# One scan for both channel tiles of a pair, and three VectorE steps one part further back in the queue

## The chip, the cores and the metric

The kernel runs on one core of one Trainium2 chip. The metric is the device time of one execution in microseconds. All data are 32-bit floats in on-chip memory (SBUF) and in the matmul accumulators (PSUM). TensorE is called PE below, VectorE DVE, ScalarE ACT, GpSimd POOL; SyncE (SP) issues most of the transfers.

## The reference

A decoder layer in three blocks, for 8 sequences of 512 tokens with 512 features: a selective state-space block (Mamba), cross-attention with 16 heads on a context of 512 tokens, and a mixture of 32 experts (4 of them chosen per token) with one shared expert; layer norms between them. The change touches the first block:

```python
x_main, z = jnp.split(layernorm(x) @ in_proj_w, 2, axis=-1)      # 1024 channels each
x_main = silu(causal_depthwise_conv1d(x_main, conv_w, conv_b))   # 4 taps
dt, B_ssm, C_ssm = split(x_main @ x_proj_w)                      # 32, 16, 16
dt = softplus(dt @ dt_proj_w + dt_proj_b)
dA  = exp(A[None, None] * dt[..., None])                         # 16 states per channel
dBx = dt[..., None] * B_ssm[:, :, None, :] * x_main[..., None]
h = dA_t * h + dBx_t                                             # step by step over the tokens
y = einsum('bdn,bn->bd', h, C_t) + x_main * D_param
out = (y * silu(z)) @ out_proj_w + x
```

In the gate of the experts, a rank of the 8 groups is computed by comparing them in pairs, and constant rows of numbers are added and multiplied in.

## The kernel before

The state-space block goes through 16 chunks: 8 sequences `b` times two halves `t` of `T` = 256 tokens. A chunk has 32 steps `k`, in the order `q`, `g`, `ci`: 4 pairs `q` of channel tiles, for each pair 4 groups `g` of 4 of the 16 states, and for each group the two channel tiles `ci` of the pair. A channel tile is 128 channels, and a tile of a step holds on its 128 partitions half of the channels for two states each, so that 4 rows of 256 tokens stand behind each other on a partition, each with one more element in front for the state carried in.

One step is made of:

- `carry` (L439): takes a buffer `h` of 4 rows of 257 elements (four such buffers in turn, `bufs=4`), and ACT copies the states carried in (or zeros, in the first half) to the front elements.
- `decays` (L433): four ACT exponentials fill one of the two tiles `l_da`, always one step ahead of its use.
- `scan` (L446): DVE multiplies `dtx` (the tile called `both` in the profile) by the broadcast states B (`bc[0]`) into `h` (L449), runs the recurrence over all 1028 elements in one scan instruction (L453; a zero of `l_da` in front of each row restarts it), and in the first half copies the 4 last states out (L455).
- `collect` (L457): DVE multiplies `h` by the broadcast states C (`bc[1]`, L470), and PE sums the states into the accumulator `py` with four matmuls (L474), which are eight records in the profile. With `g == 0` two more matmuls (L462) begin `py` with the skip connection.

After the 8 steps of a pair, `gated` (L482) multiplies the gate `zs` by `py`; there is one buffer of `py`. A buffer of `h` is free again when PE has summed it. `bcast` (L374) loads the states B and C one group ahead through SP's queue.

All else is cut into parts that run beside the scans: the input projections and convolution of the next chunk (`convolve`, L314, whose last three taps are DVE's `other_taps`, L335), the softplus of the next pair (`prepare`, L387, with its DVE part `both`, L410, which also issues eight transfers on SP's queue), the output projection, and the attention and gate of the sequence before (`units`). In attention, `maximum` (L758) makes two matmuls into a PSUM tile `ps_s` that DVE reduces to a maximum (`mx`, L768); `weigh` makes the scores `ps_t`, of which ACT makes exponentials; both share two PSUM buffers, and they take turns.

A part gives its matmuls at once and hands back what is to be done with the result. `do` (L992) runs a part and then calls `settle` (L983), which runs what the earlier parts left over; what that hands back waits for the next `settle`. So each further function handed back puts the work one part later. From this written order and its own dependencies, a scheduler in the framework makes the queue of each engine; the queues are worked off strictly in order.

Of the kernel before, what the change touches and what calls it, by code (L numbers as in the profile page):

```python
# [16 lines left out]
P = 128  # L17
# [64 lines left out]
def layers(ctx, tc, a, x1d, filld, based, xbuf):  # L82
# [73 lines left out]

    conv_tail = cp.tile([P, CC, 3], F32, name="l_conv_tail")
    state = cp.tile([P, CC, NST // NG, NG], F32, name="l_state")
    nothing = cp.tile([P, NG, 1], F32, name="l_nothing")
    nc.gpsimd.memset(nothing, 0.0)  # L160
    das = [cp.tile([P, NG, T + 1], F32, name=f"l_da{i}") for i in range(2)]
    for da in das:
        nc.gpsimd.memset(da[:, :, 0:1], 0.0)

# [23 lines left out]
        channel_multiplier=0,  # L188
    )

    early = cp.tile([P, SC, E], F32, name="l_early")
    nc.gpsimd.iota(
        early, pattern=[[0, SC], [-1, E]], base=E, channel_multiplier=0, allow_small_or_imprecise_dtypes=True
    )
    first = cp.tile([P, SC, E], F32, name="l_first")
    nc.gpsimd.iota(
        first, pattern=[[0, SC], [CAP, E]], base=-SLOTS, channel_multiplier=0, allow_small_or_imprecise_dtypes=True
    )

    taken = cp.tile([P, SC + 1, E], F32, name="l_taken")  # L200
    nc.gpsimd.memset(taken, 0.0)
# [112 lines left out]
    def convolve(t, q, f):  # L314

        c0 = 2 * q
        ps = project(f, "ps_x")

        def first_tap():
            xp = p1.tile([P, 2, T + 3], F32, tag="xp", name="xp")  # L320
            if t == 0:
                nc.gpsimd.memset(xp[:, :, 0:3], 0.0)
            else:
                nc.gpsimd.tensor_copy(xp[:, :, 0:3], conv_tail[:, c0 : c0 + 2, :])
            nc.scalar.copy(xp[:, :, 3:], ps)
            if t < S // T - 1:
                nc.gpsimd.tensor_copy(conv_tail[:, c0 : c0 + 2, :], xp[:, :, T : T + 3])
            f["xs"][q] = xs = p2.tile([P, 2, T], F32, tag="xs", name="xs", bufs=6)
            for i in range(2):
                c = c0 + i  # L330
                nc.scalar.activation(
                    xs[:, i, :], xp[:, i, 0:T], AF.Identity, bias=cb[:, c : c + 1], scale=cw[:, c, 0:1]
                )

            def other_taps():  # L335
                for i in range(2):
                    acc = xs[:, i, :]
                    for k in range(1, 4):
                        nc.vector.scalar_tensor_tensor(
                            acc, xp[:, i, k : k + T], cw[:, c0 + i, k : k + 1], acc, ALU.mult, ALU.add  # L340
                        )

            return other_taps

        return first_tap

# [27 lines left out]
    def bcast(f, g):  # L374

        got = []
        for r0 in (g * NG, NST + g * NG):
            t = bcp.tile([P, NG // 2, T], F32, tag="bc", name="bc")
            for r in range(2):
                n0 = r0 + r * NG // 2  # L380
                nc.sync.dma_start(
                    t[r * HP : (r + 1) * HP], f["scr"][n0 : n0 + NG // 2, :].partition_broadcast(HP)
                )
            got.append(t.unsqueeze(1).to_broadcast([P, 2, NG // 2, T]))
        return got

    def prepare(q, f):  # L387

        ps = psm.tile([P, 2, T], F32, tag="mm", name="ps_dt")
        for i in range(2):  # L390
            c = 2 * q + i
            nc.tensor.matmul(
                ps[:, i, :], w_dt[:, c * P : (c + 1) * P], f["xd"][0:RANK, :], start=True, stop=True
            )

        def exponentials():
# [11 lines left out]
            nc.scalar.activation(w, u, AF.Identity, bias=1.0)  # L408

            def both():  # L410

                nc.vector.scalar_tensor_tensor(w, w, -1.0, u, ALU.add, ALU.subtract)
                nc.vector.tensor_tensor(l, l, w, ALU.subtract)
                nc.vector.tensor_tensor(dt, dt, l, ALU.add)
                nc.vector.tensor_tensor(dtx, dt, f["xs"][q], ALU.mult)
                for i in range(2):
                    c = 2 * q + i
                    nc.scalar.activation(
                        f["xs"][q][:, i, :], f["xs"][q][:, i, :], AF.Identity, scale=dpar[:, c : c + 1]
                    )  # L420
                f["ready", q] = []
                for src in (dt, dtx):
                    to = p2.tile([P, 2, 2, T], F32, tag=f"both{len(f['ready', q])}", name="both")
                    for r in range(2):
                        for j in range(2):
                            nc.sync.dma_start(to[r * HP : (r + 1) * HP, :, j, :], src[j * HP : (j + 1) * HP])
                    f["ready", q].append(to)

            return both

        return exponentials

    def decays(c, g, dt, da):  # L433

        for n in range(NG):
            j, m = n // 2, n % 2
            nc.scalar.activation(da[:, n, 1:], dt[:, c % 2, j, :], AF.Exp, scale=aneg[:, c, j, g, m : m + 1])  # L437

    def carry(t, c, g):  # L439

        last = state[:, c, g].unsqueeze(2)
        h = p3.tile([P, NG, T + 1], F32, tag="h", name="h", bufs=4)
        nc.scalar.copy(h[:, :, 0:1], last if t else nothing)  # L443
        return h

    def scan(t, c, g, dtx, bc, da, h):  # L446

        steps = h.rearrange("p (j m) t -> p j m t", j=2)[:, :, :, 1:]
        nc.vector.tensor_tensor(  # L449
            steps, dtx[:, c % 2].unsqueeze(2).to_broadcast([P, 2, NG // 2, T]), bc[0], ALU.mult  # L450
        )
        flat = h.rearrange("p n t -> p (n t)")
        nc.vector.tensor_tensor_scan(flat, da.rearrange("p n t -> p (n t)"), flat, 0.0, ALU.mult, ALU.add)  # L453
        if t < S // T - 1:
            nc.vector.tensor_copy(state[:, c, g].unsqueeze(2), h[:, :, T : T + 1])  # L455

    def collect(c, g, h, bc, py, f):  # L457


        if g == 0:  # L460
            for j in range(2):
                nc.tensor.matmul(  # L462
                    py[j * HP : (j + 1) * HP, c % 2, :],
                    ident[:, j * HP : (j + 1) * HP],
                    f["xs"][c // 2][:, c % 2, :],
                    start=(c % 2 == 0),
                    stop=False,
                )
        steps = h.rearrange("p (j m) t -> p j m t", j=2)[:, :, :, 1:]
        nc.vector.tensor_tensor(steps, steps, bc[1], ALU.mult)  # L470
        for m in range(NG // 2):
            for j in range(2):
                s = (g, m, c % 2)
# [70 lines left out]
    def choose(b, x2t, pl, st):  # L544
# [13 lines left out]
        square = [P, SC, G, G]  # L558
        other = gs.unsqueeze(2).to_broadcast(square)
        own = gs.unsqueeze(3).to_broadcast(square)  # L560
        eq = gm.tile(square, F32, tag="g_eq", name="g_eq")
        nc.vector.tensor_tensor(eq, other, own, ALU.is_equal)
        nc.vector.tensor_tensor(eq, eq, lower.unsqueeze(1).to_broadcast(square), ALU.mult)
        gt = gm.tile(square, F32, tag="g_gt", name="g_gt")
# [458 lines left out]
    for i, (b, t) in enumerate(chunks):  # L1023
# [8 lines left out]
        for k, (q, g, ci) in enumerate(steps):  # L1032
            if ci == 0:
                if (q, g) != (CC // 2 - 1, NST // NG - 1):
                    bcn = bcast(f, (g + 1) % (NST // NG))
                else:
                    bcn = bcast(nf, 0) if after else None
            h = carry(t, 2 * q + ci, g)

            if k + 1 < len(steps) or after:  # L1040
                nq, ng, ni = steps[(k + 1) % len(steps)]
                decays(2 * nq + ni, ng, (f if k + 1 < len(steps) else nf)["ready", nq][0], das[(n + 1) % 2])
            scan(t, 2 * q + ci, g, f["ready", q][1], bc, das[n % 2], h)
            n += 1
            if k % 8 == 0:
                if k:
                    gated(q - 1, f, py)
                elif old:
                    gated(CC // 2 - 1, old[2], old[3])
                py = psy.tile([P, 2, T], F32, tag="py", name="py")  # L1050
            if k == 0 and old:
                twice_x(*old[:3])
            if k in (1, 2) and old:
# [365 lines left out]
```

## Time and profile before

| | |
|---|---|
| median of 3 runs | 5609.93 us (5609.75 to 5616.93) |
| the profiled execution's own time | 5620.06 us |
| its span, first to last instruction | 5617.3 us |
| busy in the span: PE / DVE / ACT / POOL | 4888.6 / 4351.5 / 2592.2 / 546.1 us |
| mean granted TensorE clock | 0.934 |

The profile counts an engine as busy while an instruction of it runs. A row of the groups gives the busy time, the mean length of one instruction in ns, and the idle time of the engine just before such instructions with what ended it. The busy time of PE is modelled and is not PE at its peak. The scans run from 84 us to 3724 us after the start; behind that lie the rest of the last sequence's attention, to about 4000 us, and then the experts and the final norm, in which nothing of the scan remains.

### The profile page before, as it was taken

What the parts mean: (1) busy time and instruction counts of PE and PEld (TensorE: products, weight loads), DVE (VectorE), ACT (ScalarE), POOL (GpSimd) and SP (SyncE); (2) the same over time, 40 slices, a digit from 0 to 9 for tenths busy, and PEclk for the clock granted to TensorE, in tenths of its full rate; (3) what the DMA queues carried; (4) which work ended last, traced back from release to release, by engine and by line L of the source; (5) the groups of instructions that cost most, each with busy time, mean ns of one, the idle gap of its engine ahead of it and who ended that gap; (6) DMA issues with size and microseconds to landing.
All of it is one profiled execution on the core that took longest, in us unless ns stands there. A gap on an engine that the chain in (4) does not pass through costs nothing. (4 is left out here: it accounts for less than half of the span.)

```text
span 5617.3 us, 60406 instructions
## 1 busy us (share of the span) xinstructions
PE 4888.6 (87%) x19752; PEld 2725.6 (49%) x19752; DVE 4351.5 (77%) x5738; ACT 2592.2 (46%) x5480; POOL 546.1 (10%) x424
## 2 busy tenths in 40 slices
PE   5667888888888988888888898879899999999994
PEld 3333344434433434443443443333577777777773
DVE  5988888989889998898989899854555655555554
ACT  4454555655556555565545656523122222222223
POOL 0000002001100200200010020010111111111111
PEclk8778999999999999999999999989899999999997
DMA  6777345434534534543463453431444444444444
GB/s 207 215 219 201 99 129 177 128 112 130 189 107 113 190 107 122 177 132 106 124 204 94 125 183 110 115 118 45 137 124 126 124 124 119 125 126 124 120 117 138
DMA packets 560426, 769.83 MB, mean 137 GB/s; under 512 B 135754, under 2 KB 268394, under 8 KB 560112
## 3 DMA queue, kind: packets, MB, share of 16 engines
q1 hardware_dynamic: 522608, 680.70, 40.2%
q0 software_dynamic: 33280, 76.90, 7.0%
q10 hardware_dynamic: 4224, 8.39, 0.4%
q8 instruction: 156, 2.56, 0.2%
q14 instruction: 158, 1.29, 0.1%
HBM read 508.68 MB, written 165.05 MB: 120 GB/s over the span
## 5 line engine op out<-in xcount | busy, mean ns | idle before, releaser
L437 ACT ACTIVATE l_da<-both,l_aneg 128x256 f32<-128x256 f32 x2048 | 888.4, 499 | 801.8 <-DVE h L453 759.7
L453 DVE TENSOR_TENSOR_SCAN h<-l_da,h 128x1028 f32<-128x1028 f32 x512 | 1171.2, 2295 | 48.5 <-ACT h L443 26.4
L474 PE MATMUL py<-h,l_twice 128*64 128x256 f32 x4096 | 628.1, 420 | 217.4 <-DVE h L470 217.3
L449 DVE TENSOR_TENSOR h<-both,bc 128x1024 f32<-128x1024 f32 x512 | 619.2, 1216 | 97.2 <-PE py L474 45.4
L470 DVE TENSOR_TENSOR h<-h,bc 128x1024 f32<-128x1024 f32 x512 | 623.5, 1220 | 6.0
L474 PEld LDWEIGHTS py<-h,l_twice 128*64 128x64 f32 x4096 | 295.3, 147 | 587.6 <-DVE h L470 260.7
L766 PE MATMUL ps_s<-l_ka,l_qa 64*128 64x512 f32 x1024 | 317.1, 699 | 142.9 <-DVE mx L768 142.7
L1199 PE MATMUL ps_h<-xT,w 128*128 128x320 f32 x1536 | 435.6, 433 | 0.0
L1279 POOL DMA_INDIRECT based<-y,xe x160 | 250.5, 1565 | 1317.2 <-ACT y L1302 579.9
L768 DVE TENSOR_REDUCE mx<-ps_s 128x2 f32<-128x1024 f32 x256 | 310.8, 1217 | 83.7 <-PE ps_s L766 82.9
L1220 DVE TENSOR_TENSOR hT<-ps_h,p 128x320 f32<-128x320 f32 x128 | 62.9, 492 | 374.7 <-PE ps_h L1199 374.6
L1199 PEld LDWEIGHTS ps_h<-xT,w 128*128 128x128 f32 x1536 | 292.4, 191 | 118.4 <-issue 0.8
L792 PE MATMUL ps_t<-l_qa,l_ka 64*128 64x512 f32 x1024 | 302.0, 654 | 15.8 <-ACT eT L796 11.9
L796 ACT ACTIVATE eT<-ps_t 128x1024 f32<-128x1024 f32 x256 | 259.1, 1013 | 111.9 <-PE ps_t L792 111.5
L808 PE MATMUL po<-eT,l_va 128*64 128x512 f32 x1024 | 279.2, 623 | 23.0 <-ACT raw L820 19.0
L1199 PE MATMUL ps_h<-t,s 128*128 128x320 f32 x1024 | 286.1, 432 | 0.0
L641 POOL DMA_INDIRECT xbuf<-x2t,dest x128 | 216.7, 1693 | 622.1 <-DVE dest L635 583.7
L305 PE MATMUL ps_z<-xnT,wm 128*128 128x256 f32 x1024 | 246.3, 395 | 31.2 <-DMA wm<-in_in_proj_w 28.4
L503 PE MATMUL po<-wm,zs 128*128 128x512 f32 x512 | 246.7, 634 | 13.0 <-DMA wm<-in_out_proj_w 8.5
L703 PE MATMUL ps_p<-x2T,wa 128*128 128x512 f32 x512 | 244.7, 627 | 11.1 <-DVE hT L883 9.1
L305 PE MATMUL ps_x<-xnT,wm 128*128 128x256 f32 x1024 | 245.3, 393 | 1.4 <-ACT xnT L294 1.1
L305 PEld LDWEIGHTS ps_z<-xnT,wm 128*128 128x128 f32 x1024 | 196.2, 196 | 83.7 <-ACT l_da L437 27.1
(225 smaller groups left out, 7397.0 us busy)
## 6 DMA issues: line engine op xcount, KB each, us to landing
bc<-scr SPq DMA_DIRECT2D x1024, 128.0 KB
w<-in_w SPq DMA_DIRECT2D x96, 1024.0 KB
wm<-in_in_proj_w SPq DMA_DIRECT2D x128, 512.0 KB
xbuf<-zero SPq DMA_DIRECT2D x32, 1362.5 KB
xe<-xbuf SPq DMA_DIRECT2D x32, 1362.5 KB
both<-dt SPq DMA_DIRECT2D x256, 128.0 KB
both<-dtx SPq DMA_DIRECT2D x256, 128.0 KB
wm<-in_out_proj_w SPq DMA_DIRECT2D x64, 512.0 KB
```

The costliest lines, as they stand in the source:

```text
L305: nc.tensor.matmul(ps[:, i, :], w[:, dc, i * P : (i + 1) * P], f["xnT"][:, dc, :], start=(dc == 0), stop=(dc == DC - 1),)
L437: nc.scalar.activation(da[:, n, 1:], dt[:, c % 2, j, :], AF.Exp, scale=aneg[:, c, j, g, m : m + 1])
L449: nc.vector.tensor_tensor(steps, dtx[:, c % 2].unsqueeze(2).to_broadcast([P, 2, NG // 2, T]), bc[0], ALU.mult)
L453: nc.vector.tensor_tensor_scan(flat, da.rearrange("p n t -> p (n t)"), flat, 0.0, ALU.mult, ALU.add)
L470: nc.vector.tensor_tensor(steps, steps, bc[1], ALU.mult)
L474: nc.tensor.matmul(py[j * HP : (j + 1) * HP, c % 2, :], twice, h[:, j * 2 + m, 1:], start=False, stop=(s == (NST // NG - 1, NG // 2 - 1, 1)),)
L766: nc.tensor.matmul(ps[:, j, :], qa[r, lt * P : (lt + 1) * P], ka[r, :], start=True, stop=True)
L768: return lambda: nc.vector.tensor_reduce(mx[:, lt, :].unsqueeze(2), ps, AX.X, ALU.max) and None
L792: nc.tensor.matmul(ps[:, j, :], ka[r, kc * P : (kc + 1) * P], qa[r, :], start=True, stop=True)
L796: nc.scalar.activation(eT, ps, AF.Exp)
L808: nc.tensor.matmul(po[j * 2 * HD : (j + 1) * 2 * HD, :], va[:, kc, i, j * HD : (j + 2) * HD], eT[:, j, :], start=(kc == 0), stop=(kc == SC ...
L1199: nc.tensor.matmul(ps, w[:, n, r * P : (r + 1) * P], x[:, n, :], start=not more and n == 0, stop=n == 1, skip_group_check=more,)
```

## The change

Five things are edited.

1. `carry`, `decays` and `scan` work on both channel tiles of a pair at once, at every even `k`: `h` and `l_da` have 8 rows of 257 elements, there are two buffers of `h` instead of four, and two of `l_da` as before. The decays are computed one pair of steps ahead. `collect` is as before, once for each channel tile, on half of `h`.
2. `other_taps` and `both` are handed back through one more function, so they come one part later.
3. `gated` stands just ahead of `collect`, behind the parts of the step, and not just behind the scan.
4. `prepare` is called at `k % 8 == 2`, not 3.
5. The constants `early` and `first` hold one row that is broadcast, and the two comparison tiles of the gate lie in one buffer of the shared tag `row`.

```diff
-    nothing = cp.tile([P, NG, 1], F32, name="l_nothing")
+    none = cp.tile([P, 2, NG], F32, name="l_none")
...
-    das = [cp.tile([P, NG, T + 1], F32, name=f"l_da{i}") for i in range(2)]
+    das = [cp.tile([P, 2 * NG, T + 1], F32, name=f"l_da{i}") for i in range(2)]
...
-    early = cp.tile([P, SC, E], F32, name="l_early")
...
+    early = early.unsqueeze(1).to_broadcast([P, SC, E])
...
-            return other_taps
+            return lambda: other_taps
...
-            return both
+            return lambda: both
...
+    def decays(q, g, dt, da):
+
+        for i in range(2):
+            for n in range(NG):
+                j, m = n // 2, n % 2
+                nc.scalar.activation(
+                    da[:, i * NG + n, 1:], dt[:, i, j, :], AF.Exp, scale=aneg[:, 2 * q + i, j, g, m : m + 1]
+                )
...
-        h = p3.tile([P, NG, T + 1], F32, tag="h", name="h", bufs=4)
-        nc.scalar.copy(h[:, :, 0:1], last if t else nothing)
+        h = p3.tile([P, 2 * NG, T + 1], F32, tag="h", name="h", bufs=2)
+        nc.scalar.copy(h.rearrange("p (i n) t -> p i n t", i=2)[:, :, :, 0], last(q, g) if t else none)
...
+        steps = h.rearrange("p (j m) t -> p j m t", m=NG // 2)[:, :, :, 1:]
+        both = [P, 4, NG // 2, T]
         nc.vector.tensor_tensor(
-            steps, dtx[:, c % 2].unsqueeze(2).to_broadcast([P, 2, NG // 2, T]), bc[0], ALU.mult
+            steps,
+            dtx.rearrange("p i j t -> p (i j) t").unsqueeze(2).to_broadcast(both),
+            bc[0].to_broadcast(both),
+            ALU.mult,
         )
         flat = h.rearrange("p n t -> p (n t)")
         nc.vector.tensor_tensor_scan(flat, da.rearrange("p n t -> p (n t)"), flat, 0.0, ALU.mult, ALU.add)
         if t < S // T - 1:
-            nc.vector.tensor_copy(state[:, c, g].unsqueeze(2), h[:, :, T : T + 1])
+            nc.vector.tensor_copy(last(q, g), h.rearrange("p (i n) t -> p i n t", i=2)[:, :, :, T])
...
+        h = h[:, c % 2 * NG : (c % 2 + 1) * NG]
         steps = h.rearrange("p (j m) t -> p j m t", j=2)[:, :, :, 1:]
-        nc.vector.tensor_tensor(steps, steps, bc[1], ALU.mult)
+        nc.vector.tensor_tensor(steps, steps, bc[1].to_broadcast([P, 2, NG // 2, T]), ALU.mult)
...
-        eq = gm.tile(square, F32, tag="g_eq", name="g_eq")
+        both = p3.tile([P, D], F32, tag="row", name="g_eq").rearrange("p (n j g h) -> p n j g h", n=2, j=SC, g=G)
+        eq, gt = both[:, 0], both[:, 1]
...
-            h = carry(t, 2 * q + ci, g)
-
-            if k + 1 < len(steps) or after:
-                nq, ng, ni = steps[(k + 1) % len(steps)]
-                decays(2 * nq + ni, ng, (f if k + 1 < len(steps) else nf)["ready", nq][0], das[(n + 1) % 2])
-            scan(t, 2 * q + ci, g, f["ready", q][1], bc, das[n % 2], h)
-            n += 1
-            if k % 8 == 0:
-                if k:
-                    gated(q - 1, f, py)
-                elif old:
-                    gated(CC // 2 - 1, old[2], old[3])
-                py = psy.tile([P, 2, T], F32, tag="py", name="py")
+            if ci == 0:
+                h = carry(t, q, g)
+
+                if k + 2 < len(steps) or after:
+                    nq, ng, _ = steps[(k + 2) % len(steps)]
+                    decays(nq, ng, (f if k + 2 < len(steps) else nf)["ready", nq][0], das[(n + 1) % 2])
+                scan(t, q, g, f["ready", q][1], bc, das[n % 2], h)
+                n += 1
...
-            if k % 8 == 3:
+            if k % 8 == 2:
                 if q + 1 < CC // 2:
                     do(prepare, q + 1, f)
...
             settle()
+            if k % 8 == 0:
+                if k:
+                    gated(q - 1, f, py)
+                elif old:
+                    gated(CC // 2 - 1, old[2], old[3])
+                py = psy.tile([P, 2, T], F32, tag="py", name="py")
             collect(2 * q + ci, g, h, bc, py, f)
```

More of the change, by code (lines that the diff above doesn't have):

```diff
@@ L158, in layers @@
     state = cp.tile([P, CC, NST // NG, NG], F32, name="l_state")
-    nothing = cp.tile([P, NG, 1], F32, name="l_nothing")
-    nc.gpsimd.memset(nothing, 0.0)
-    das = [cp.tile([P, NG, T + 1], F32, name=f"l_da{i}") for i in range(2)]
+    none = cp.tile([P, 2, NG], F32, name="l_none")
+    nc.gpsimd.memset(none, 0.0)
+    das = [cp.tile([P, 2 * NG, T + 1], F32, name=f"l_da{i}") for i in range(2)]
     for da in das:
@@ L189, in layers @@
     )
-    early = cp.tile([P, SC, E], F32, name="l_early")
[L192 to L198, printed above, removed]
+    early = cp.tile([P, E], F32, name="l_early")
+    nc.gpsimd.iota(early, pattern=[[-1, E]], base=E, channel_multiplier=0, allow_small_or_imprecise_dtypes=True)
+    early = early.unsqueeze(1).to_broadcast([P, SC, E])
+    first = cp.tile([P, E], F32, name="l_first")
+    nc.gpsimd.iota(first, pattern=[[CAP, E]], base=-SLOTS, channel_multiplier=0, allow_small_or_imprecise_dtypes=True)
+    first = first.unsqueeze(1).to_broadcast([P, SC, E])
     taken = cp.tile([P, SC + 1, E], F32, name="l_taken")
@@ L383, in bcast @@
                 )
-            got.append(t.unsqueeze(1).to_broadcast([P, 2, NG // 2, T]))
+            got.append(t.unsqueeze(1))
         return got
@@ L427, in both, with carry, last, scan @@
                     f["ready", q].append(to)
-            return both
+            return lambda: both
         return exponentials
[L433 to L441, printed above, removed]
-        h = p3.tile([P, NG, T + 1], F32, tag="h", name="h", bufs=4)
-        nc.scalar.copy(h[:, :, 0:1], last if t else nothing)
-        return h
-    def scan(t, c, g, dtx, bc, da, h):
-        steps = h.rearrange("p (j m) t -> p j m t", j=2)[:, :, :, 1:]
+    def decays(q, g, dt, da):
[5 more added lines that the diff above has]
+                )
+    def carry(t, q, g):
+        h = p3.tile([P, 2 * NG, T + 1], F32, tag="h", name="h", bufs=2)
+        nc.scalar.copy(h.rearrange("p (i n) t -> p i n t", i=2)[:, :, :, 0], last(q, g) if t else none)
+        return h
+    def last(q, g):
+        return state[:, 2 * q : 2 * q + 2, g]
+    def scan(t, q, g, dtx, bc, da, h):
+        steps = h.rearrange("p (j m) t -> p j m t", m=NG // 2)[:, :, :, 1:]
+        both = [P, 4, NG // 2, T]
         nc.vector.tensor_tensor(
-            steps, dtx[:, c % 2].unsqueeze(2).to_broadcast([P, 2, NG // 2, T]), bc[0], ALU.mult
+            steps,
+            dtx.rearrange("p i j t -> p (i j) t").unsqueeze(2).to_broadcast(both),
+            bc[0].to_broadcast(both),
+            ALU.mult,
         )
@@ L560, in choose @@
         own = gs.unsqueeze(3).to_broadcast(square)
-        eq = gm.tile(square, F32, tag="g_eq", name="g_eq")
+        both = p3.tile([P, D], F32, tag="row", name="g_eq").rearrange("p (n j g h) -> p n j g h", n=2, j=SC, g=G)
+        eq, gt = both[:, 0], both[:, 1]
         nc.vector.tensor_tensor(eq, other, own, ALU.is_equal)
         nc.vector.tensor_tensor(eq, eq, lower.unsqueeze(1).to_broadcast(square), ALU.mult)
-        gt = gm.tile(square, F32, tag="g_gt", name="g_gt")
         nc.vector.tensor_tensor(gt, other, own, ALU.is_gt)
```

## The prediction, made before the changed kernel ran

> **What bounds the kernel now.** I read the windows first, to see which stage the change reaches. All scans lie between 84 and 3724 us:
>
> ```profile
> core 0: us, PE busy (x) PEld busy (x) DVE busy (x) ACT busy (x) POOL busy (x), PEclk, DMA share, GB/s
> 84.00:3724.00 3640.00, 3094.19 (x12620) 1479.61 (x12620) 3299.42 (x3751) 2041.92 (x4353) 252.52 (x190) 0.92 0.49 144
> ```
>
> VectorE is busy for 3299 of 3640 us (91%), TensorE for 3094 (85%), ScalarE for 56%. So a microsecond off VectorE's queue counts here if TensorE follows, and nothing after 3724 us can change. Next the groups, for what a step costs:
>
> ```profile
> L453 DVE TENSOR_TENSOR_SCAN h<-l_da,h 128x1028 f32<-128x1028 f32 x512 | 1171.2, 2295 | 48.5 <-ACT h L443 26.4
> L449 DVE TENSOR_TENSOR h<-both,bc 128x1024 f32<-128x1024 f32 x512 | 619.2, 1216 | 97.2 <-PE py L474 45.4
> L455 DVE COPY l_state<-h 128x4 f32<-128x4 f32 x256 | 42.1, 166 | 2.9
> L413 DVE TENSOR_TENSOR l<-l,dtx 128x512 f32<-128x512 f32 x64 | 44.1, 688 | 1.0
> ```
>
> Then the waits of VectorE in those 3640 us (total, times, longest), to see what its 341 idle us are:
>
> ```profile
> DVE h L449 <- PE py L474: 45.4, 27, 3.7
> DVE zs L486 <- PE py L474: 40.2, 19, 4.3
> DVE xs L339 <- ACT xs L331: 33.0, 21, 4.7
> DVE dtx L412 <- ACT dtx L408: 27.0, 7, 5.2
> DVE h L449 <- DMA both<-dtx: 26.8, 15, 7.1
> DVE h L453 <- ACT h L443: 26.4, 16, 2.0
> ```
>
> No single wait rules. Two of them, 45.4 and 26.4 us, are the ring of `h` buffers: the multiply, or the ScalarE copy ahead of it, stands until TensorE has summed an old buffer. Three others (40.2, 33.0 and 27.0) belong to the instructions that edits 2 and 3 put back. Last the timeline, for how VectorE's instructions follow each other:
>
> ```profile
> 1583.17 1.22 DVE L449 TENSOR_TENSOR h<-both,bc 128x1024 f32<-128x1024 f32 x1
> 1584.49 2.30 DVE L453 TENSOR_TENSOR_SCAN h<-l_da,h 128x1028 f32<-128x1028 f32 x1
> 1586.82 0.17 DVE L455 COPY l_state<-h 128x4 f32<-128x4 f32 x1
> 1587.03 1.23 DVE L470 TENSOR_TENSOR h<-h,bc 128x1024 f32<-128x1024 f32 x1
> 1588.17 1.22 DVE L768 TENSOR_REDUCE mx<-ps_s 128x2 f32<-128x1024 f32 x1
> 1589.31 1.22 DVE L449 TENSOR_TENSOR h<-both,bc 128x1024 f32<-128x1024 f32 x1
> 1589.44 1.13 PE L766 MATMUL ps_s<-l_ka,l_qa 64*128 64x512 f32 x4 [1.84 <-DVE mx L768]
> 1590.62 2.30 DVE L453 TENSOR_TENSOR_SCAN h<-l_da,h 128x1028 f32<-128x1028 f32 x1
> 1592.84 1.20 DVE L768 TENSOR_REDUCE mx<-ps_s 128x2 f32<-128x1024 f32 x1
> 1594.15 1.22 DVE L470 TENSOR_TENSOR h<-h,bc 128x1024 f32<-128x1024 f32 x1
> ```
>
> In attention VectorE has no gap, and TensorE waits for each reduction (1.84 us here): VectorE is the bound. An instruction that does not need the one before it starts before that one ends: after 1.14 us behind one of 1.23 (L470 to L768), after 2.22 us behind a scan of 2.30 (1590.62 to 1592.84). One that needs it starts later: 1.32 us from a multiply to its own scan, 2.33 from a scan to its own copy, 0.21 from a copy to its own product.
>
> **Term 1, fewer instructions.** 512 multiplies, 512 scans and 256 copies become 256, 256 and 128; the elements stay. The slope of a multiply is (1216 - 688) / 512 = 1.031 ns, so 1024 elements take 1.056 us, and of the 1.14 us between starts 0.08 are fixed. The scan overlaps its follower by the same 0.08, so I give it the same fixed part; no other length of scan is in the trace. Saved: 256 x 0.16 = 41 us; 128 copies at 0.07 (1505.17 to 1505.24, after a copy that nothing behind it needs) are 9. Then the dependent pairs. In the order of instructions a scan stands right behind its own multiply 164 times before and 117 after, a copy behind its own scan 86 and 39, a product behind its copy 97 and 68, or behind its scan 79 and 67. At 0.18, 0.11, 0.14 and 0.11 us that is 8.5 + 5.2 + 4.1 + 1.3 = 19. Sum 69 us. Bounds: 50 without the dependencies; by full lengths 256 x (0.16 + 0.16) + 128 x 0.166 = 103. I take 69, since starts are what a full queue is made of.
>
> The Trainium skill ("VectorE: DVE Perf Modes", the section on the DRAIN) says that the next operation waits until the pipe is empty. The 1.14 us behind an instruction of 1.23 speak against that for independent ones; by that rule this term alone would be the 103, and the forecast 5507 us.
>
> **Term 2, steps put back.** The waits of `zs`, `xs` and `dtx` are 40.2 + 33.0 + 27.0 = 100 us. One part later, ScalarE or TensorE has had one part's time more; mean waits are 2.1, 1.6 and 3.9 us, and a part of attention is about 1.1 us of TensorE (the `ps_s` row), a projection longer. I take half, 50 us, between 0 and 100. The eight transfers issued behind the softplus go with it: what queues behind them on SP are the loads of B and C (11 us of waits today) and weights. `both` is called one step earlier and handed back one part later, so I book nothing; if the cover goes, today's 26.8 us at the multiply double.
>
> **Term 3, the ring of `h`.** Four buffers of a step become two of a pair, in the same memory. A multiply of step k today needs the sum of step k-4; the merged one needs k-3 as well as k-4. I paired all 254 even steps in the trace: 154 multiplies start before the sum of k-3 is done (plus 0.4 us for the copy), short by 808 us in total. That is a ceiling and not a price: the new order puts the multiply further back. In it 60 of 254 (24%) multiplies stand behind an instruction that proves the needed sum, against 163 of 508 (32%) before. Behind a waiting multiply stand the scan, the products and the reductions that TensorE waits for. Bounds: 0 more (half as many chances to wait) to 808. Today's rows, 45.4 + 26.4 = 72, are nearest; I take half as much again, +35.
>
> **Term 4, longer blocks.** A reduction that falls behind multiply and scan now stands up to 2 x (1.06 + 2.14) + 0.16 = 6.6 us, against 3.4. TensorE's waits for reductions are 142.7 us (L766, 82 times) and 44.6 (L775, 39 times) over the whole span. Each could grow by 1.6 us, half the difference: 121 x 1.6 = 194 us. Where VectorE has no gap that is no loss; I take +15, between 0 and 194.
>
> The Trainium skill ("Perfetto Trace Analysis", on optimizing Scalar/DVE operations) advises to break instructions up where an unsaturated VectorE leaves bubbles on other engines. At 91% busy this stage is near the other case of the same section, where grouping helps; by the warning term 4 would be the full 194, and the time 5720 us.
>
> **At nothing.** ScalarE's copies halve (256 x 0.192 us = 49) and its exponentials stay 2048, in blocks of 3.4 us and not 1.7; it idles 759.7 us before them now, waiting for old scans, and that slack covers it. Without it, each block would hold a softmax exponential 1.7 us longer. The gate's buffers run 8 times; a wait for `row` would cost one copy of 0.6 us each.
>
> **The sum.** -69 - 50 + 35 + 15 = -69 us. The profiled execution takes 5620.06 us (2.8 around its span of 5617.3) and would take 5551; the median of the runs is 10.1 lower, so 5541 us.
>
> **The rivals.**
> *The ring decides (slower).* VectorE stands at the merged multiply for sums that TensorE's queue holds behind attention matmuls. For it: at 1596.43 the multiply of a step began 0.19 us after the sum of k-4 ended (1596.24), and the sum of k-3 ended only at 1602.83. Against it: the reordering, and 72 us today. Other terms give -69 - 50 + 15 = -104, so it decides from 104 / 808 = 13% of the shortage. At a fifth, 162 us: +58, 5668 us.
> *Nothing moves.* VectorE's queue is shorter, but TensorE sets the pace: the low ends, -50, are given back by +50 of terms 3 and 4: 5610 us. For it: 85% busy and waits at `py`; against it: the attention stretch.
> *All of it.* Full lengths and all three waits: -103 - 100 = -203, 5407 us. Against it: VectorE, once freed, runs into TensorE.
>
> **Chances.** Forecast 0.54 (own range 5490 to 5595), all of it 0.12, nothing 0.08, ring 0.26. What a measurement of this kernel can tell from no change is about 0.2%, 11 us. Faster 0.66, same 0.08, slower 0.26. Range 5440 to 5665: it leaves out half of each outer case, 0.19 in all.
>
> **What would show it.** After: scans of about 4.43 us x256 and multiplies of 2.27; VectorE's busy time down by about 100 us; `xs`, `zs` and `dtx` waits near 50 together; multiply and ScalarE-copy waits near 107. Waits for `py` above 170 would show the ring rival; waits of L766 and L775 doubled with gaps on VectorE, term 4 mis-sized. Scans above 4.6 us would refute term 1.

## The result, and the profile after

The changed kernel takes 5624.3 us (median of 20 runs, 5604.98 to 5641.48), the kernel before in the same runs 5615.06 us (20 runs, 5609.75 to 5622.26): the ratio is 1.0016, with a 95% interval of 1.0009 to 1.0023. The forecast of 5541 us was wrong: nothing was gained, and if anything 9 us were lost. The profiled execution took 5629.23 us, its span 5627.5 us, at a mean granted clock of 0.94.

The scans now end at 3737 us and not at 3724. The window of the whole scan stage, with the columns of the one shown before:

```profile
84.00:3737.00 3653.00, 3085.47 (x12612) 1483.74 (x12612) 3245.96 (x3115) 1948.65 (x4062) 239.37 (x190) 0.93 0.49 144
```

VectorE is busy for 3246 us and no longer 3299: 53 us less, with 640 instructions fewer in the whole span (5738 to 5098). The stage is 13 us longer all the same, so VectorE's idle time grew from 341 to 407 us, by 66. The work went, and waiting took its place. The groups show that the instructions have the lengths that were expected:

```profile
L460 DVE TENSOR_TENSOR_SCAN h<-l_da,h 128x2056 f32<-128x2056 f32 x256 | 1135.8, 4437 | 13.8 <-ACT h L443 1.2
L453 DVE TENSOR_TENSOR h<-both,bc 128x2048 f32<-128x2048 f32 x256 | 584.5, 2287 | 152.0 <-PE py L482 89.8
L462 DVE COPY l_state<-h 128x8 f32<-128x8 f32 x128 | 21.2, 165 | 1.3
```

VectorE's waits in this stage (total, times, longest) name where it now stands:

```profile
DVE h L453 <- PE py L482: 89.8, 62, 3.9
DVE xs L337 <- ACT xs L329: 48.4, 25, 6.5
DVE mx L776 <- PE ps_s L774: 47.7, 23, 3.9
DVE h L453 <- DMA both<-dtx: 46.3, 8, 7.3
DVE g_m L558 <- ACT g_sc L557: 36.2, 6, 9.9
DVE dtx L410 <- ACT dtx L406: 16.8, 10, 2.2
DVE zs L494 <- PE py L482: 15.4, 12, 1.7
```

The moved steps gained at `zs` (40.2 before) and `dtx` (27.0), but `xs` rose from 33.0, the transfer behind the softplus (`both<-dtx`) from 26.8, the reductions `mx` from 13.1, and `g_m`, the gate's wait for ScalarE, is new. The ring of `h` (89.8 and 1.2 at the scan, 91 together) rose from 72. And TensorE's waits in the same stage:

```profile
PE py L482 <- DVE h L478: 122.1, 40, 11.6
PE ps_s L774 <- DVE mx L776: 67.5, 49, 2.9
PE ps_p L711 <- DVE attT L849: 48.5, 7, 7.3
PE ps_t L800 <- ACT eT L804: 35.3, 35, 2.8
```

and in the kernel before:

```profile
PE py L474 <- DVE h L470: 212.0, 68, 15.1
PE ps_s L766 <- DVE mx L768: 141.9, 80, 4.4
```

The waits for the products (`py`) and the reductions (`ps_s`) became much smaller. But `attT`, the last step of attention's division, rose from 7.5 us (longest 1.3) to 48.5 (longest 7.3), and `eT`, the softmax exponentials, from 10.2. The timeline shows one of the former:

```profile
1769.22 4.43 DVE L460 TENSOR_TENSOR_SCAN h<-l_da,h 128x2056 f32<-128x2056 f32 x1
1773.57 0.67 DVE L849 SCALAR_TENSOR_TENSOR attT<-attT,total 128x512 f32<-128x512 f32 x1
1774.29 3.64 PE L711 MATMUL ps_p<-wa,attT 128*128 128x512 f32 x4 [7.25 <-DVE attT L849]
```

A division of 0.67 us stands behind a scan of 4.43 us, and TensorE stands 7.25 us for it. The last experiment shows that this is the place of the division in the queue, and not the length of the scan: with two short scans in place of the long one, the wait is as long.

### The profile page after: what moved, and what is told of

Its sections match the earlier page's. It is cut to its first block, busy times and chain, and to the rows that moved or that the text cites. A ratio compares the mean times of both kernels' runs of the same rounds, so it can differ in the third digit from the quotient of the medians.

```text
span 5627.5 us, 59332 instructions
## 1 busy us (share of the span) xinstructions
PE 4880.0 (87%) x19752; PEld 2730.3 (49%) x19752; DVE 4298.1 (76%) x5098; ACT 2498.3 (44%) x5186; POOL 532.9 (9%) x424
## 5 line engine op out<-in xcount | busy, mean ns | idle before, releaser
L460 DVE TENSOR_TENSOR_SCAN h<-l_da,h 128x2056 f32<-128x2056 f32 x256 | 1135.8, 4437 | 13.8 <-ACT h L443 1.2
L436 ACT ACTIVATE l_da<-both,l_aneg 128x256 f32<-128x256 f32 x2048 | 866.9, 497 | 554.5 <-DVE h L460 502.0
L453 DVE TENSOR_TENSOR h<-both,bc 128x2048 f32<-128x2048 f32 x256 | 584.5, 2287 | 152.0 <-PE py L482 89.8
L478 DVE TENSOR_TENSOR h<-h,bc 128x1024 f32<-128x1024 f32 x512 | 612.2, 1218 | 4.9 <-DVE l_state L462 0.3
L482 PEld LDWEIGHTS py<-h,l_twice 128*64 128x64 f32 x4096 | 307.4, 145 | 478.6 <-issue 223.2
L774 PE MATMUL ps_s<-l_ka,l_qa 64*128 64x512 f32 x1024 | 300.1, 662 | 79.9 <-DVE mx L776 68.3
L816 PE MATMUL po<-eT,l_va 128*64 128x512 f32 x1024 | 296.0, 650 | 25.4 <-ACT eT L804 20.6
L303 PE MATMUL ps_z<-xnT,wm 128*128 128x256 f32 x1024 | 253.2, 403 | 35.2 <-DMA wm<-in_in_proj_w 29.3
```

What stands on the lines that cost most here:

```text
L303: nc.tensor.matmul(ps[:, i, :], w[:, dc, i * P : (i + 1) * P], f["xnT"][:, dc, :], start=(dc == 0), stop=(dc == DC - 1),)
L436: nc.scalar.activation(da[:, i * NG + n, 1:], dt[:, i, j, :], AF.Exp, scale=aneg[:, 2 * q + i, j, g, m : m + 1])
L453: nc.vector.tensor_tensor(steps, dtx.rearrange("p i j t -> p (i j) t").unsqueeze(2).to_broadcast(both), bc[0].to_broadcast(both), ALU.mult,)
L478: nc.vector.tensor_tensor(steps, steps, bc[1].to_broadcast([P, 2, NG // 2, T]), ALU.mult)
L482: nc.tensor.matmul(py[j * HP : (j + 1) * HP, c % 2, :], twice, h[:, j * 2 + m, 1:], start=False, stop=(s == (NST // NG - 1, NG // 2 - 1, 1)),)
L774: nc.tensor.matmul(ps[:, j, :], qa[r, lt * P : (lt + 1) * P], ka[r, :], start=True, stop=True)
```

## The experiments

A ratio is always to the kernel before in the same runs, with its 95% interval; us worked out from a ratio take 0.1% as 5.6 us, and a difference of two ratios is uncertain by some 6 to 12 us. The scheduler makes a new order of the queues for every edited kernel, unless the text says that the order was held.

### The edits taken apart

**Moves alone** (edits 2, 3 and 4 on the kernel before).

> Edits 2, 3 and 4 alone, on the kernel before, with single steps and four buffers of h. Theory A: slower by 40 to 60 us, ratio 1.007 to 1.011. Theory B: faster by 20 to 50 us, ratio 0.991 to 0.996, as the waits of zs, xs and dtx (100 us) fall by half. Theory C: within 0.2%, other waits in their place.

Measured: 5605.04 us, 0.9977 (0.9969 to 0.9986): 13 us gained. The waits of `zs` fell from 40.2 to 5.3 us and `xs` from 33.0 to 23.0, but one grew, in VectorE's waits of this kernel:

```profile
DVE h L449 <- DMA both<-dtx: 72.3, 13, 8.6
```

It was 26.8. Counted in waits, what the softplus's later place adds at the multiply is most of what the others save; that it costs this much of the time is not borne out below, where the softplus is handed back directly.

**Merge alone** (edits 1 and 5).

> Edits 1 and 5 alone: the merged scan with its rings, but taps, softplus, gate product and prepare where they were. Theory A (VectorE sets the pace; its saving of some 66 us is real and the steps put back by edits 2 to 4 bring new stalls, such as the 46 us at the merged multiply for both<-dtx): about 5565 us, ratio 0.991. Theory B (VectorE sets the pace; the saving is taken back by the ring of h and the long blocks, which edit 1 brings itself): 5615 to 5650 us, ratio 1.000 to 1.006, since the waits of xs, zs and dtx come back too. Theory C (VectorE does not set the pace, so its saving becomes idle time): within 0.3% of before, and VectorE's idle time up by some 65 us.

Measured: 5696.37 us, 1.0135 (1.012 to 1.015): 76 us lost, which is above all three expected ranges. VectorE's busy time fell by 43 us (4351.5 to 4308.9) and its idle time in the scan stage rose from 341 to 462 us (window of 3719 us, busy for 3257). So edits 1 and 5, pairing and merging together, are what loses, and not for VectorE's own work.

**Pair ring without merged instructions.** The buffers, the decays and the copy of the carried states stay as changed; multiply, scan and state copy are issued for each channel tile:

```diff
-        nc.vector.tensor_tensor(steps, ...)             # 2048 elements
-        nc.vector.tensor_tensor_scan(flat, ...)         # 2056
+        for i in range(2):
+            h, d = whole[:, i * NG : (i + 1) * NG], da[:, i * NG : (i + 1) * NG]
...
+            nc.vector.tensor_tensor(steps, ...)         # 1024
...
+            nc.vector.tensor_tensor_scan(flat, ...)     # 1028
```

> The changed kernel with its rings of pairs and its written order, but two multiplies, two scans and two copies per pair again, each on half of h. It has the ring and the order of the change without the saved instructions and with short blocks. Theory A or B with the fixed cost of an instruction real: slower than the changed kernel by 50 to 70 us (5680 us, ratio 1.011 against before). If the long blocks are what takes the saving back: equal to the changed kernel or faster (5600 to 5625 us). Theory C: within 0.3% of the changed kernel, with VectorE's idle time lower by some 65 us.

Measured: 5626.92 us, 1.0009 (1.0000 to 1.0018). And the same without the moves:

> The pair rings with two multiplies, two scans and two copies per pair, and taps, softplus, gate product and prepare where they were before. Against the merged run without the moves (1.0135): if the long blocks of the merged instructions cost the 1.35%, this one is at 1.000 to 1.005; if the pair rings and the decays a pair ahead cost it, this one is at 1.010 to 1.016.

Measured: 5657.94 us, 1.0072 (1.0059 to 1.0086). That lies between the two expected ranges: neither the long blocks nor the pair rings alone make the 1.35%. The six kernels make a table of ratios:

| | no moves | with moves |
|---|---|---|
| single steps, four buffers | 1 | 0.9977 |
| pairs, split instructions | 1.0072 | 1.0009 |
| pairs, merged instructions | 1.0135 | 1.0016 |

Read down: going over to pairs costs 40 us without the moves and 18 with them, and merging the instructions on top costs 35 more without the moves and 4 with them, which can't be told from nothing. Each of the six has its own order of the queues. Read across: the moves bring 13, 35 and 67 us. The table holds a surprise in VectorE's busy time: it falls from 4350.5 to 4307.7 us when the steps are paired and still split (with moves), and only by 10 more (to 4298.1) when they are merged. Why, the last experiment shows.

### Does a microsecond of VectorE count?

**Additions that nothing needs**, 512 of 128 columns, in the kernel before; first free to go anywhere, then bound to their step by reading its broadcast states:

```diff
+        c_ = bc[1][:, 0, 0, 0:128]
+        nc.vector.tensor_tensor(spare, c_, c_, ALU.add)
```

> The kernel before with one more addition of 128 columns per step on VectorE, between multiply and scan, that nothing needs and that needs nothing (512 of them, about 0.13 + 0.08 = 0.21 us each, estimated from the rows of before; up to 0.1 us of each hides in the gap between a multiply and its own scan). It measures how much of VectorE's work reaches the end. If VectorE sets the pace (A, B): 55 to 110 us more, ratio 1.010 to 1.020. Theory C: less than 30 us more, ratio under 1.005.

> As the run with the extra addition of 128 columns per step, but the addition reads the broadcast C of its own step, so that it can't run far ahead (there all 512 stood in the first four chunks, and 46 of the 50 us were lost in chunks 0 to 3). 512 additions of about 0.21 us from start to start, 108 us in all, spread over all chunks. If VectorE sets the pace: +70 to +108 us, ratio 1.012 to 1.019. If TensorE with the queues around it sets the pace (theory C): +10 to +40 us, most of it in the first three chunks, ratio 1.002 to 1.007, with VectorE's idle time in a later chunk down by about 6 us.

Measured: free 5669.89 us, 1.0088 (1.0074 to 1.0101), but the scheduler had put them all into the first chunks, so this says little of the stage. Bound: 5666.93 us, 1.0092 (1.0077 to 1.0107). Busy time rose by 88 us (4351.5 to 4439.8), the time by 52. That is 59%, but not the price of work alone: the additions read states that a transfer brings, and VectorE stood 69.5 us in front of them for it.

**The same additions in the changed kernel**, two behind each merged multiply, and **the state copies left out of the kernel before**:

> The changed kernel with 512 further additions on VectorE, 128 columns each, two behind each multiply, on the broadcast states of the same step: 88 us more of VectorE's busy time, as in the same experiment on the kernel before, where 50 us of it reached the end. If VectorE's saved 66 us became slack that stands idle, the additions fill it first: under 20 us, below 5645 us. If the idle time is made of waits that no further work can fill, it costs as much as before, about 50 us: 5674 us.

> The kernel before without the 256 state copies of VectorE (L455); the states carried into each second half are zeros, so this part of the recurrence is left out. VectorE loses 42 us of busy time, nothing else changes in the ring or in the length of the blocks. Theory B (a microsecond off VectorE reaches the end at 57%, as a microsecond on it did): 5615 - 24 = 5591 us. Theory C (an asymmetry: work added to VectorE costs, work taken off becomes idle time, since TensorE and VectorE wait for each other in turn): within 8 us of before, 5607 to 5617 us.

Measured with the additions: 5715.33 us, 1.0174 (1.0158 to 1.0189). Against the changed kernel that is 1.58%, 89 us, for 83 us more of busy time (4298.1 to 4381.1). That looks as if its 407 us of idle time could take no further work, but the additions brought a wait of their own, the largest of VectorE's in this kernel:

```profile
DVE l_spare L462 <- DMA bc<-scr: 123.7, 46, 5.4
```

The scan stage has 404 us of idle time here, of which these are 124; the rest fell to 280. So this run doesn't tell whether work that waits for nothing would have filled the idle time.

Measured without the copies: 5611.73 us, 0.9986 (0.9977 to 0.9995): 8 us gained, of 27 us less busy time. On the kernel before, then, 30% of the work taken off reached the end; the 59% of the work added can't be set against it because of the additions' own waits. None of these rows is free of the scheduler, which made another order each time.

### The ring and the neighbours

**Three and five buffers** of `h` instead of four, in the kernel before (`bufs=3`, `bufs=5`):

> The kernel before with three buffers of h and not four: the multiply of step k needs the sum of step k-3, as the merged one does. If the depth of the ring is what takes the saving back (theory B): +40 to +100 us, ratio 1.007 to 1.018. If not: within 0.3%.

> The kernel before with five buffers of h. Its waits at the ring are 45 us on VectorE's multiply and 26 us on the scan behind ScalarE's copy. If VectorE sets the pace and the ring holds it: faster by 30 to 70 us, ratio 0.988 to 0.995. If something else sets the pace: within 0.2%, with other waits in place of these.

Measured: three 5657.29 us, 1.0075 (1.0062 to 1.0089); five 5733.29 us, 1.0206 (1.0192 to 1.022). With three, the ring's waits rose from 72 to 111 us (59.1 at the multiply, 52.2 at ScalarE's copy) and the time by 42. With five they were 19 us, and the kernel was the slower one by far: VectorE stood 95.7 us for `both<-dtx` and 70.6 for `xs`. With another depth the scheduler makes another order, and the runs don't separate the two; the ring's own waits, at any rate, do not set the time alone.

**Exponentials in two halves**, four at the even step and four at the odd one; **softplus handed back directly** as before (`return both`), in the changed kernel, in the moves alone, and with the former:

> The changed kernel, but ScalarE's eight exponentials of a pair are given four at the even step and four at the odd one (and behind the scan in the written order), so that they no longer stand as one block of 3.4 us in ScalarE's queue. In the changed kernel TensorE waits 35 + 20 us for the softmax exponentials eT and 23 us for the normed rows x2t, against 10 + 4 + 1 before. If ScalarE's blocks take the saving back: faster than the changed kernel by 30 to 60 us, ratio 0.991 to 0.996. If they don't (VectorE's long blocks and the ring do): within 0.2% of the changed kernel's 1.0016.

> The changed kernel, but the softplus on VectorE handed back directly again (its part of edit 2 undone), while prepare stays at the earlier step. The changed kernel waits 46 us at the multiply for both<-dtx, 7 us once in each even chunk. If that wait is on the path: faster by 25 to 45 us, ratio 0.993 to 0.997. If other waits take its place: within 0.2% of 1.0016, and the wait for dtx<-ACT (16.8 us) grows.

> The kernel before with the moved taps, the moved gate product and prepare at the earlier step, but the softplus handed back directly. Against the run with all moves (0.9977), whose wait for both<-dtx was 72 us: if that wait counts, 0.989 to 0.994; if the time is set elsewhere, 0.996 to 0.999.

> The changed kernel with the split exponentials and with the softplus handed back directly. If both waits count and add up: 0.983 to 0.991, which would beat every version so far. If the pair rings and VectorE's long blocks hold the time: 0.998 to 1.003.

Measured: exponentials in halves 5650.76 us, 1.0065 (1.0052 to 1.0078), slower than the changed kernel; softplus direct 5614.08, 0.9996 (0.9988 to 1.0005), 11 us better than the changed kernel; moves without it 5603.71, 0.9971 (0.9961 to 0.9982), not to be told from the moves with it; both 5651.87, 1.0058 (1.0046 to 1.0071). Both together are about as slow as the exponentials in halves alone. Whether the later place of the exponentials costs this or the new order that came with it, these runs don't tell.

### Which instruction, and length or order?

**Only the multiply split, or only the scan split**, in the changed kernel:

> The changed kernel with the merged multiply split into two of 1024 elements; the scan and the state copy stay merged. VectorE gets 256 x 0.08 = 20 us more of instruction starts. Theory A (the long instructions cost what they save, because what stands behind them waits): the block is cut once, so most of what the splitting costs is given back: within 5 us of the changed kernel (5619 to 5629 us). Theory B (VectorE's time counts at about 57%, and the ring of pairs alone takes the gain back): +12 us, 5636 us.

> The changed kernel with the merged scan split into two of 1028 elements; the multiply and the state copy stay merged. The scans cost 256 x (2 x 2.295 - 4.437) = 39 us more of busy time, or 20 us more of starts. Theory A (the 4.4 us block is what makes others wait): no slower than the changed kernel, 5610 to 5626 us. Theory B (VectorE's time counts at about 57%): +11 to +22 us, 5635 to 5646 us.

Measured: multiply split 5760.55 us, 1.0248 (1.0234 to 1.0262); scan split 5630.27 us, 1.0018 (1.0009 to 1.0027). By the ratios the split scan costs 1 us against the changed kernel, as the first theory expected of it; but neither theory had room for 130 us from 256 short multiplies. So the order itself had to be held. The order of each engine's queue in the changed kernel was written out, and every instruction chained behind the one ahead of it; the second half of a split instruction stands directly behind the first:

```diff
+            ins = nc.vector.tensor_tensor_scan(flat, d, flat, 0.0, ALU.mult, ALU.add)
+            if i:
+                SECOND.add(ins.ins.name)
...
+        for one, two in zip(queue, queue[1:]):
+            tc.add_manual_dep(two, one.name, dep, reason="order")
```

> The changed kernel with only the multiply split in two, as in the run that took 5760.55 us, but with every engine's queue chained in the changed kernel's own order. If the 133 us of that run came from the order that the scheduler made around the shorter multiplies, this one costs only its 256 x 0.08 = 20 us of starts, less what is idle: 5627 to 5652 us. If the shorter multiplies themselves cost it, it stays above 5730 us.

> The changed kernel with the multiply, the scan and the state copy split in two each, and with every engine's queue chained in the changed kernel's own order: the second half of each stands directly behind the first, nothing else moves. VectorE gets the fixed parts back: 256 x 0.16 + 128 x 0.07 = 50 us of starts, and its busy time rises by about 66 us. Theory V (VectorE sets the pace, merging saves, and only the new order took the saving away): +28 to +50 us on the changed kernel, 5655 to 5675 us. Theory W (the saving does not reach the end even in the same order): within 10 us of the changed kernel, 5617 to 5637 us.

Measured with the multiply split: 5663.07 us, 1.0076 (1.0062 to 1.0089). The same instructions in the scheduler's own order took 5760.55, so 97 us lie between the two orders. The time is above the 5652 us that the expectation allowed: of the remaining 34 us against the changed kernel, the 256 x 0.07 us of starts make 18, and the rest is not accounted for. The changed kernel itself was not run with its queues chained, so what the chaining costs by itself is not measured.

Measured with all three split: 5593.97 us (5587.51 to 5596.12), 0.9952 (0.9939 to 0.9966). That is 0.9936 of the changed kernel (0.992 to 0.995, from the two ratios), 36 us less, where one theory had 28 to 50 more and the other no difference. It is the fastest kernel of the study, 0.48% ahead of the one before; the moves alone, without the softplus's, are 0.29% ahead. Its scan stage:

```profile
84.00:3701.00 3617.00, 3059.36 (x12612) 1484.22 (x12612) 3259.24 (x3754) 1967.15 (x4069) 198.36 (x190) 0.93 0.50 145
```

The same instructions in the same places, in 639 more pieces: VectorE is busy for 13 us more than in the changed kernel, idle for 49 less (358 against 407). The split kernel of the table (with the moves) has the same split instructions in the scheduler's own order, and takes 1.0009: 32 us more. Two things stand behind the gain in the held order.

First, the split costs VectorE next to nothing when the halves alternate. In the kernel before, a scan directly behind its own multiply starts 1.32 us after it, since it needs its result; two multiplies start 1.135 us apart. In multiply, multiply, scan, scan no instruction needs the one directly ahead of it: the scan starts 1.135 us behind the second multiply, the scans 2.209 us apart, and the follower 2.190 behind them, 6.67 us in all. Merged, a scan directly behind its own multiply (118 of 256 stand so) starts 2.394 us after it and its follower 4.358 later, 6.75 us. The split pairs of the table mostly stand in this alternating order too (133 of 256 directly so), which fits their busy time of 4307.7 us.

Second, what the scan frees and feeds comes earlier. The timeline at the same place of the queue, of the changed kernel:

```profile
1743.69 4.44 DVE L460 TENSOR_TENSOR_SCAN h<-l_da,h 128x2056 f32<-128x2056 f32 x1
1748.16 2.11 ACT L436 ACTIVATE l_da<-both,l_aneg 128x256 f32<-128x256 f32 x5 [2.66 <-DVE h L460]
1752.94 1.09 ACT L329 ACTIVATE xs<-xp,l_cb,l_cw 128x256 f32<-128x256 f32 x2
1753.57 2.19 DVE L337 SCALAR_TENSOR_TENSOR xs<-xp,l_cw,xs 128x256 f32<-128x256 f32 x5 [3.04 <-ACT xs L329]
```

and of the kernel with all split and the order held:

```profile
1728.25 4.49 DVE L461 TENSOR_TENSOR_SCAN h<-l_da,h 128x1028 f32<-128x1028 f32 x2
1730.58 1.71 ACT L436 ACTIVATE l_da<-both,l_aneg 128x256 f32<-128x256 f32 x4 [0.40 <-DVE h L461]
1736.56 1.09 ACT L329 ACTIVATE xs<-xp,l_cb,l_cw 128x256 f32<-128x256 f32 x2
1737.19 2.20 DVE L337 SCALAR_TENSOR_TENSOR xs<-xp,l_cw,xs 128x256 f32<-128x256 f32 x5 [2.21 <-ACT xs L329]
```

The exponentials overwrite the tile that the scan reads. Behind one long scan the first starts 4.47 us after the scan's start (1748.16 - 1743.69), behind two short ones after 2.33, when half of the tile is free. The first part of the convolution (`xs`, L329) stands behind them in ScalarE's queue, and the taps (L337) wait for it: they start 9.88 us after the scan in the one and 8.94 in the other. Over the whole stage, ScalarE's wait at `l_da` for the scan, from its waits in the two kernels, the changed one first:

```profile
ACT l_da L436 <- DVE h L460: 502.0, 143, 8.3
```

```profile
ACT l_da L436 <- DVE h L461: 273.5, 159, 5.7
```

VectorE's wait for `xs` falls with it from 48.4 to 30.1 us, TensorE's for `eT` from 35.3 to 18.5. The kernel with only the multiply split is the control for this: its queues are chained in the same order, and the two differ by the splitting of the scan and the state copy alone. With the scan still in one piece its waits stay as in the changed kernel, 44.0 us for `xs`, 35.2 for `eT`, and

```profile
ACT l_da L436 <- DVE h L460: 514.1, 140, 8.4
```

It takes 5663.07 us against 5593.97: splitting the scan there gains 69 us (ratio 0.988, 0.986 to 0.990). Part of that is VectorE's own: two multiplies and a scan directly behind them leave the scan waiting for the second one, 1.32 us and not 1.135 behind it. That is 6.81 us in place of 6.67, 0.14 for each of some 118 pairs, 17 us. So most of the gain goes with the earlier release of `l_da`. What the split doesn't touch is the division behind the scan:

```profile
PE ps_p L717 <- DVE attT L855: 51.6, 7, 7.4
```

That wait was 48.5 us with the long scans. One more thing differs, TensorE's granted clock: 0.943 in the kernel with all split, 0.940 in the changed one, 0.936 with only the multiply split, and TensorE's busy time in the scan stage goes with it (3059, 3085 and 3096 us). Whether the clock is a cause of the shorter time or follows from it, no run tells.

## Why the prediction was wrong, by its own steps

The forecast was -69 us and the measured change +9, so 78 us are missing. By the table, 37 of them are the moves (-13 where -50 was booked), and 41 are pairs and merged instructions together (+22 where terms 1, 3 and 4 booked -19).

**Term 1** had the lengths right and the reach wrong. Scans of 4.43 us and multiplies of 2.27 came as said (4437 and 2287 ns); VectorE's busy time fell by 53 us where it said 100. That saving comes from pairing, and hardly from merging: with the steps paired and the instructions still split, 43 of the 53 are there. And it was booked as if all of it reached the end, "since starts are what a full queue is made of". It did not: over the scan stage, 53 us less work became 66 us more idle time.

**Term 4** is the step whose mechanism failed. It booked +15 for longer blocks, between 0 and 194, and looked for the loss at the reductions. Those waits fell (`ps_s` from 141.9 to 67.5). The long block costs elsewhere: at ScalarE, which does not overwrite `l_da` before the whole scan is done (502.0 us of waits against 273.5), and in what stands behind that in its queue. The prediction had put ScalarE's longer blocks and its waits for old scans at nothing, since that slack would cover them. In the changed kernel's own order, two short instructions in place of each long one are 36 us faster at almost the same busy time. In orders that the scheduler makes for each form the difference does not show (1.0016 merged, 1.0009 split), so the 36 us are the price in this order and not in every one. The Trainium skill ("Perfetto Trace Analysis", the section on optimizing Scalar/DVE operations) sets the two cases against each other: group where the engine is saturated, break up where it leaves bubbles on other engines. The prediction took VectorE, at 91% busy, for the first. The 36 us say that in this order it was the second; the page names no size.

**Terms 3 and 1 together.** Pairing brings the ring, booked at +35, and with it most of VectorE's saving, as the table shows. Measured is +18 with the moves, +40 without. The ring's waits themselves came out near what was said, 91 us against 107. How much of the rest is the ring and how much the order that the scheduler made for pairs stays open: where the same instructions ran in two orders, 97 and 32 us lay between them.

**Term 2** booked -50. On single steps the moves bring 13 us, on merged pairs 67. The waits of `zs`, `xs` and `dtx`, 100 us before, are 81 after, where it said 50: `xs` grew. The softplus's transfers, booked at nothing with the remark that the 26.8 us double if the cover goes, rose to 46.3. Handed back directly, 11 us return in the changed kernel, and on single steps nothing that can be told (0.9971 against 0.9977). So this is a small part of the 37 us; why the lower waits of the others did not bring more stays open.

**The rivals.** The ring did not decide: its sign was 170 us of waits for `py`, and there are 91. "Nothing moves" had nearly the right time, 5610 us, and a reason that fell: TensorE does not set the pace alone, for with its instructions and their order unchanged the splitting of VectorE's scan moved the time by 69 us. It was terms 1 and 2 that were given back, by more than the 50 us that it allowed. "All of it" was far off.

**The method.** Each term was priced in the trace of before as if the rest of the order would stay. The change of one length rearranges every queue, and that alone was worth up to 97 us here, more than any term of the sum.

## What to carry to other kernels

Fewer and longer instructions pay only by their fixed part, 0.07 to 0.08 us each here, and two independent halves that alternate with the next step hide the dependency just as well; so first look who waits for the end of the long instruction, and whose buffer it holds until then. Where a scheduler makes the queues, compare an edit in a held order before you believe what it costs: the same instructions took 5663 and 5761 us in two orders. And when you add work to see whether an engine's idle time is slack, look first whether the added work itself waits: here the additions waited 124 us for a transfer, and the test told little.

## What was unexpected of the hardware

- An instruction that needs its predecessor's result starts about 0.19 us later than one that does not (1.32 against 1.135 us behind a multiply), and one independent instruction between them takes that away entirely: the scan of the first half, behind the second half's multiply, starts 1.135 us after it. With the scan in one piece, which needs the second multiply too, it is 1.32 again.
- A kernel with one more buffer in the ring was 2.06% slower, with another order of its queues; no run holds the order to tell the two apart.
- TensorE's granted clock went roughly with the time: between 474 and 3600 us it was 0.92 in the kernel of 5760.55 us, 0.94 in the one of before and 0.95 in the one of 5593.97; but it was 0.95 in the changed kernel too, which is no faster than the one before. Which of the two follows the other, no run tells.
